# A fused AdaLN and routed low-rank FFN kernel: the first block's second stage in the two-level form of the others

## The chip, the cores and the metric

One core of one Trainium2 chip runs the whole kernel. The metric is the device time of one execution in microseconds (us), as a median over runs; smaller is better. Engines are called by the profile's names: PE is TensorE (matmul), DVE is VectorE, ACT is ScalarE, POOL is GpSimd, SP is SyncE (here a DMA queue only).

## The reference

Inputs are `x` (64 x 64 x 512), `cond` (64 x 256) and the weights, all fp32. Cut to what is computed:

```python
q = relu(cond @ W3 + b3)                          # one row of 512 per batch
v = (64 * x + x.sum(axis=1, keepdims=True)) * q[:, None, :]
y = relu(v @ W2 + b2)                             # first stage
base = y @ W_base + b_base                        # second stage
shared = (y @ A_s) @ B_s
gates = softmax(y @ W_router + b_router)          # 6 experts
w = the two largest gates, others 0
routed = sum over e of w[e] * (y @ A_r[e]) @ B_r[e]   # rank 16
out = x + base + shared + routed
```

## The kernel before

**Blocks.** The 4096 tokens are worked in four blocks (`k` = 0 to 3) of 1024. Features lie on partitions in four chunks of 128; a block's tokens are split into two halves of 512 columns. So v, y and the result of a block are each a 2 x 2 matrix of quarters: a pair of chunks by a half of the tokens (y11, y12 are the two chunk pairs of the first half, y21, y22 those of the second).

**Fewer products.** A product of 2 x 2 quarters is made with seven products instead of eight (Winograd's form): sums of quarters are formed first, four on the side of the rows (`row_sums`, L272) and four on the side of the weights (`weight_sums`, L134), then products numbered 1 to 7 are accumulated in PSUM. `seed` copies on ACT start a bank from another bank's value, since sums of products are shared. The same can be done once more inside a product: each of the seven is then itself made of seven products of 128 x 128 weights with 256 columns ("two levels"). It needs inner sums of both sides: `inner_row_steps` (L342) and `inner_weight_side` (L148), four instructions each.

**First stage.** Block 0 uses `first_mixed` (L397): plain products for half of the tokens and one level for the rest. It also starts block 1's preparation. Blocks 1 to 3 use `first_inner` (L480), two levels throughout.

**Second stage.** The loop at L1324 computes `ph`, which holds y's products with the low-rank and router weights. Then:
- block 0 calls `second` (L874): one level, seven products of four 512-column matmuls each, the routed part added in PSUM, x added by DVE out of PSUM, the result sent by SP's queue.
- blocks 1 and 2 call `second_between` (L714): products 1, 2, 4, 5 and 3 on two levels, products 6 and 7 on one. Products 6 and 7 are added to x on DVE and stored; the five others are left in SBUF by ACT copies and DVE additions and then added in DRAM by an accumulating DMA from POOL's queue (`to_rows`, L743).
- block 3 calls `second_inner`.

Inside, `gate` (L659) forms the softmax and the top two on DVE with one Exp on ACT, `weigh` (L636) multiplies them into `hw`, `turn` (L645) transposes `hw` on PE, and `difference` (L654) subtracts its halves on POOL. In `second_between` some products and their copies are issued between the gate's instructions (`first`, L793).

**Order by hand.** Every engine runs its instructions in the order in which the program issues them. The preparation of the next block (scaling x in place, 64 instructions on ACT, some on DVE; sums; row sums; inner sums) is cut into steps that wait in two lists: `behind`, drawn by `fill(n)`, and `held`, drawn by `sums_ahead(n)`. `prepare` (L302) fills the lists; for k = 1 it puts everything into `behind`, together with the sums of W_base (`tb_steps`) and part of the inner sums of W2 (`inner_steps[4:]`). In `second`, a helper `share` draws from `behind` in even portions. The inner sums of W_base are on POOL: `low_t` and `bcat_d` in `second` (the list `beside`), `wide["steps"]` around block 1's first stage.

Of the kernel before, what the change touches and what calls it, by code (L numbers as in the profile page):

```python
# [38 lines left out]
def adaln_ffn(ctx: ExitStack, tc: tile.TileContext, xa, x0, x1, head, w3, w2, wb, a, bcat, bb, br, outT):  # L39
# [80 lines left out]
    wb_sb = load_weight(wb, "wb_sb")  # L120
    bcat_sb = const.tile([GB, D], F32, tag="bcat_sb", name="bcat_sb")
    nc.sync.dma_start(bcat_sb[:GR], bcat)
    load_x(1)
    nc.sync.dma_start(bcat_sb[GR:], bb)
# [79 lines left out]
    def modulate(k):  # L204
# [18 lines left out]
        def batch(c, b):  # L223
            x = v[:, c, :, ts(b, NH)]
            scale, bias = nq[:, c, b : b + 1], vsum[:, c, b : b + 1]
            if k > 1 and c == CHUNKS[-1] and b >= BB // 2:
                nc.vector.tensor_scalar(x, x, scale, bias, ALU.mult, ALU.add)
            else:
                nc.scalar.activation(x, x, AF.Identity, bias=bias, scale=scale)  # L229
# [72 lines left out]
    def prepare(k, also=()):  # L302
# [8 lines left out]
        def row_step(c, n):  # L311
            if not made:
                ss[k], row_steps = row_sums(vs[k], "s")
                made.extend(
                    row_steps(slice(c, c + 1), nc.gpsimd if k > 1 and c == KH - 1 else nc.vector) for c in range(KH)
                )
            made[c][n]()
# [4 lines left out]
        among = [((4, 4 if k == 1 else 5), sums[c1])]  # L322
        if k == 1:
            among += [((25, 27, 29, 31), early), ((16, 16), sums[c2]), ((19, 20), sums[c3])]
        for places, steps in among:
            for n, step in reversed(list(zip(places, steps))):
                pairs[n].insert(0, step)
        for n, step in enumerate(also):
            pairs[n if n < 4 else 12 + n].append(step)
        behind.extend([step] for step in sums[c0])  # L330
        if k == 1:
            behind.extend(pairs)
            behind.extend([step] for step in late + prepare_inner(k))
        else:


            n = len(pairs) - BB // 4
            behind.extend(pairs[:n])
            first, inner_sums = prepare_inner(k, late[3])
            held.extend(sums[c2] + sums[c3] + early + first + sum(pairs[n:], []) + late[:3] + inner_sums)  # L340
# [9 lines left out]
    def prepare_inner(k, fourth=None):  # L350
# [30 lines left out]
        all_of, soon, third = slice(0, 4), slice(0, 3), slice(3, 4)  # L381
        late = []
        if fourth:
            late += [fourth] + steps("sums", of_s(third), nc.gpsimd, third)
            all_of = soon
        late += steps("two", of(0), nc.gpsimd)
        if fourth:
            late += [lambda: last_part.pop()()]
        late += steps("four", of(1), nc.gpsimd)
        inner[k] = dict(s=side, e3=lambda: s["e3"], places=late_places, late=late)  # L390
        inner_sums = steps("sums", of_s(all_of), nc.vector, all_of)
        return (first, inner_sums) if fourth else first + inner_sums
# [4 lines left out]
    def first_mixed(y):  # L397
# [52 lines left out]
        for step in t2_steps + inner_steps[:4] + s_steps():  # L450
            step()
        prepare(1, tb_steps + inner_steps[4:])
# [5 lines left out]
        for j in range(KH):  # L458
# [19 lines left out]
            fill(1)  # L478

# [220 lines left out]
    def load_rows(k):  # L700

        res = {}
        for n, (f, h) in zip(pair_tags[2:3] + pair_tags[:2] + pair_tags[3:], ((1, 0), (1, 1), (0, 0), (0, 1))):
            if (f, h) == (0, 0) and 0 < k < NB - 1:

                nc.sync.dma_start(outT[k, :KH, h], x1[k, :KH, :, ts(h, TB)])
                continue
# [6 lines left out]
    def second_between(k, y, res):  # L714
# [69 lines left out]
        for o in (1, 2):  # L784
            inner_sums(o)

        def main_part(ph):
            open_banks(1)
# [23 lines left out]
            fill(2)  # L812
            tools.take_u(1)
            sums_ahead(2)
            for j in range(KH):
                seed(j, "z", bank["y", j])
                with_x(x12, "y", j, KH, 0)
                if j == 0:
                    fill(2 if k == 1 else 1)

            for o in (5, 4):
                inner_sums(o)
            fill(2)
# [6 lines left out]
            fill(2)  # L830
# [5 lines left out]
            hws["less"] = difference(k, hwT)[:GB]  # L836
            inner_sums(3)
# [6 lines left out]
            fill(1)  # L844
# [4 lines left out]
            fill(1)  # L849
            sixth(3)  # L850
            fill(1)
# [3 lines left out]
            start(4)  # L855
            seventh(3)
            sums_ahead(2)
            second_and_third(3)
            sixth(4)
            ends(3)  # L860
# [12 lines left out]

    def second(k, y, ph, res):  # L874

        sy = sys_[k]
        ps = {}

        def bank(name, j):
            ps[name, j] = ps_p.tile([P, TB], F32, tag="pp", name=f"o{name}_{k}_{j}")  # L880
            return ps[name, j]

        def prod(i, j, name, start=True):
            product(bank(name, j) if start else ps[name, j], i, j, tb, sy, start=start)

        def seed(name, source, j):
            nc.scalar.copy(bank(name, j), ps[source, j])

        def row(f, h):
            return res[f // KH, h][:, f % KH]  # L890

        def with_x(name, j, f, h):

            t = row(f, h)
            nc.vector.tensor_tensor(t, ps[name, j], t, ALU.add)
            return t

        def routed(name, j, f, hw):
            nc.tensor.matmul(
                ps[name, j], bcat_sb[:, ts(f, P)], hw, start=False, stop=True, skip_group_check=True  # L900
            )

        def finish(name, j, f, h):
            nc.sync.dma_start(outT[k, f, h], with_x(name, j, f, h))

        def leave(p, f, h, add):
            nc.vector.tensor_tensor(add, p, add, ALU.add)
            nc.sync.dma_start(outT[k, f, h], add)


        places = list(range(9, 0, -1))
        most = {9: 4, 8: 5, 7: 6}

        def share():
            n = places.pop(0)
            left = len(behind) - 13
            fill(min(left, most.get(n, 6)) if left > 0 else -(-len(behind) // n))

        u12, u22 = {}, {}
        gate(k, ph)  # L920
        prod(1, 0, "x")
        seed("y", "x", 0)
        prod(1, 1, "x")
        seed("y", "x", 1)
        prod(6, 0, "y", start=False)
        seed("z", "y", 0)
        prod(2, 0, "x", start=False)
        weigh(k, ph)
        u12[0] = with_x("y", 0, KH, 0)
        share()  # L930
        prod(7, 0, "z", start=False)
        u22[0] = with_x("z", 0, KH, 1)
        prod(6, 1, "y", start=False)
        seed("z", "y", 1)
        u12[1] = with_x("y", 1, KH + 1, 0)
        share()
        prod(2, 1, "x", start=False)
        prod(7, 1, "z", start=False)
        u22[1] = with_x("z", 1, KH + 1, 1)
        hwT = turn(k)  # L940
        hwd = difference(k, hwT)
        for step in beside:
            step()
        share()
        prod(4, 0, "z", start=False)
        prod(5, 0, "w")
        share()
        routed("x", 0, 0, hwT[:GB, 0])
        finish("x", 0, 0, 0)
        routed("z", 0, 0, hwT[:GB, 1])  # L950
        finish("z", 0, 0, 1)

        routed("w", 0, KH, hwT[:GB, 1])
        leave(ps["w", 0], KH, 1, u22[0])
        share()
        prod(5, 1, "w")
        routed("w", 1, KH + 1, hwT[:GB, 1])
        leave(ps["w", 1], KH + 1, 1, u22[1])
        share()
        routed("x", 1, 1, hwT[:GB, 0])  # L960
        finish("x", 1, 1, 0)
        share()
        prod(4, 1, "z", start=False)
        routed("z", 1, 1, hwT[:GB, 1])
        finish("z", 1, 1, 1)
        share()
        prod(3, 0, "w", start=False)
        routed("w", 0, KH, hwd[:GB])
        leave(ps["w", 0], KH, 0, u12[0])
        share()  # L970
        prod(3, 1, "w", start=False)
        routed("w", 1, KH + 1, hwd[:GB])
        leave(ps["w", 1], KH + 1, 0, u12[1])
# [101 lines left out]
    def second_inner(k, y, res):  # L1075
# [196 lines left out]
    sys_, inner = {}, {}  # L1272
# [4 lines left out]
        w2_sb, t2, [(all_t[:, :, a:b], o, nc.vector) for a, b, o in ((0, 4, (5, 6, 7, 4)), (4, 6, (1, 2)), (6, 7, (3,)))]  # L1277
    )
    inner_steps = sum(inner_steps, [])
# [3 lines left out]
    low_side, low_steps = inner_weights(wb_sb, tb, [(low_t, (1, 2), nc.gpsimd)])  # L1283
# [3 lines left out]
    beside = [lambda: nc.gpsimd.tensor_tensor(bcat_d, bcat_pairs[:, :, 0], bcat_pairs[:, :, 1], ALU.subtract)]  # L1287
    beside += low_steps[0]
# [10 lines left out]
    for k in range(NB):  # L1299
# [5 lines left out]
        else:  # L1305
            if k == 1:
                for step in wide["steps"][0]:
                    step()
            rest = first_inner(k, y)
            if k == 1:  # L1310
                for step in wide["steps"][1]:
                    step()
# [10 lines left out]
        two = second_inner(k, y, res) if k == NB - 1 else second_between(k, y, res) if k else None  # L1323
        for n, (h, s) in enumerate(groups):  # L1324
            if rest and n == 0:
                sums_ahead(2)
            if rest and n == 2:
                rest()
                two["sums"]()
            if two and n in two:  # L1330
                if n == 6:
                    fill(4)
                two[n]()
                if n == 7:
# [6 lines left out]
        if two:  # L1341
            two["all"](ph)
            continue
        sys_[k], steps = row_sums(y, "sy")
        for step in steps():
            step()
# [53 lines left out]
```

## Time and profile before

The median of three runs is 253.76 us (252.5 to 253.93).

| | before |
|---|---|
| profiled execution, its own time | 253.81 us |
| its span in the trace | 252.0 us |
| TensorE's mean granted clock | 0.999 |
| busy: PE, DVE, ACT, POOL | 98%, 81%, 63%, 50% |
| block 0, second stage (window 34.21 to 73.15): busy PE, DVE, ACT, POOL | 38.94, 35.34, 23.59, 10.49 us of 38.94 |
| block 1, second stage (window 94.07 to 131.59): busy PE, DVE, ACT, POOL | 37.52, 35.47, 27.83, 22.56 us of 37.52 |

Times inside the trace count from the start of the span; the profiled execution lasted 1.8 us longer than its span. A line of a timeline gives the start, the length, the engine, the line of the kernel, the operation, what it writes from what it reads, the shapes and the count; the brackets at its end say how long the engine was idle before it and what ended that. The chain that ended last gives start, length and the work that set the pace there. A 4-byte matmul is recorded as two instructions.

### The profile page before, as it was taken

The page shows a single profiled execution, that of the slowest core. Times are in us where ns is not written, and L with a number is a line of the kernel's source. Part 1 is how long each engine was busy: PE and PEld are TensorE (multiplying, and loading weights), DVE is VectorE, ACT ScalarE, POOL GpSimd, SP SyncE. Part 2 cuts the span into 40 slices and gives each one's busy share as a digit, 9 for nine tenths or more (in the row PEclk, how much of TensorE's full clock was granted, in tenths as well). Part 3 has the DMA queues.
Part 4 walks back from the last instruction along what each step waited for, and adds up shares of the span by engine and source line. Part 5 has one row for each costly group of instructions (what it writes and reads, how often), then busy time and mean ns, then how long its engine had stood idle before and what let it go on. Part 6 is the DMA issues. An engine that isn't in the chain of part 4 may idle for free.

```text
span 252.0 us, 3678 instructions
## 1 busy us (share of the span) xinstructions
PE 246.8 (98%) x1134; PEld 189.4 (75%) x1134; DVE 203.8 (81%) x407; ACT 158.0 (63%) x436; POOL 126.2 (50%) x150
## 2 busy tenths in 40 slices
PE   8999999999999999999999999999999999999993
PEld 3846897454468889857888889947888889966783
DVE  2899998879996988999995778999992576797472
ACT  2299588579018889797638889796826428252310
POOL 1000000009707579059469968339659894059850
PEclk9999999999999999999999999999999999999999
DMA  6997818000431024835459922306259852500054
GB/s 181 370 350 274 330 28 307 0 3 16 151 125 42 3 86 138 336 147 216 61 80 195 156 94 101 127 25 250 28 79 197 138 133 97 166 1 0 9 194 134
DMA packets 17482, 33.82 MB, mean 134 GB/s; under 512 B 1605, under 2 KB 3781, under 8 KB 17462
## 3 DMA queue, kind: packets, MB, share of 16 engines
q1 hardware_dynamic: 13910, 27.09, 30.3%
q0 software_dynamic: 3264, 6.29, 15.9%
q10 hardware_dynamic: 288, 0.20, 0.3%
q8 instruction: 9, 0.15, 0.2%
q14 instruction: 11, 0.09, 0.1%
HBM read 19.94 MB, written 14.68 MB: 137 GB/s over the span
## 4 chain that ended last, share of the span: by engine, by line
PE 96%; DMA 2%; DVE 0%; SPq 0%; issue 0%
PE ia L502 14%; PE ph L1337 11%; PE ib L502 11%; PE ha L987 10%; PE hb L987 8%; PE oz L181 7%; PE py L409 6%; PE oy L181 6%; PE ja L987 4%; PE jb L987 3%; PE ox L181 3%; PE ow L181 3%; DMA w_sb<-in_w_dram 2%; PE yw L181 1%; PE pt L649 1%; PE yz L181 1%
## 5 line engine op out<-in xcount | busy, mean ns | idle before, releaser
L229 ACT ACTIVATE x<-x,vsum,nq 128x64 f32<-128x64 f32 x176 | 63.3, 431 | 1.4 <-DVE vsum L221 1.4
L656 POOL TENSOR_TENSOR hwd<-hwT 113x512 f32<-113x512 f32 x4 | 5.1, 1271 | 55.4 <-ACT hwT L651 55.4
L1337 PEld LDWEIGHTS ph<-a_sb,y 128*128 128x128 f32 x256 | 30.7, 192 | 0.8
L1337 PE MATMUL ph<-a_sb,y 128*128 128x118 f32 x256 | 30.7, 275 | 0.0
L493 DVE TENSOR_TENSOR u<-ib,u 128x256 f32<-128x256 f32 x42 | 16.4, 418 | 11.9 <-PE ib L502 11.8
L493 DVE TENSOR_TENSOR u<-ia,u 128x256 f32<-128x256 f32 (+1 forms) x36 | 16.1, 462 | 7.1 <-ACT u L540 5.8
L508 ACT COPY ib<-ia 128x256 f32<-128x256 f32 x21 | 7.6, 361 | 17.2 <-PE ia L502 17.2
L395 ACT ACTIVATE y<-u,head_sb 128x256 f32<-128x256 f32 (+1 forms) x30 | 15.8, 583 | 3.7 <-DVE u L468 3.0
L502 PE MATMUL ib<-inner_s,inner_t 128*128 128x256 f32 x60 | 17.4, 379 | 0.0
L219 DVE TENSOR_REDUCE vsum<-x 128x8 f32<-128x512 f32 x24 | 15.5, 676 | 0.0
L181 PE MATMUL oz<-sy,tb 128*128 128x512 f32 x32 | 15.0, 592 | 0.0
L409 PE MATMUL py<-v,w_sb 128*128 128x512 f32 (+1 forms) x40 | 14.4, 510 | 0.6 <-DMA w_sb<-in_w_dram 0.6
L181 PE MATMUL oy<-sy,tb 128*128 128x512 f32 x32 | 14.7, 597 | 0.0
L511 ACT COPY ib<-ib 128x256 f32<-128x256 f32 x21 | 7.6, 360 | 9.0 <-PE ib L502 8.6
L502 PEld LDWEIGHTS ib<-inner_s,inner_t 128*128 128x128 f32 x60 | 11.4, 190 | 1.6
L409 PEld LDWEIGHTS py<-v,w_sb 128*128 128x128 f32 x40 | 7.4, 190 | 6.7 <-issue 4.8
L344 POOL TENSOR_TENSOR sy<-sy 128x256 f32<-128x256 f32 x4 | 3.8, 952 | 17.2 <-PE oy L181 17.2
L267 ACT ACTIVATE v<-x,vsum,nq 128x64 f32<-128x64 f32 x32 | 11.0, 429 | 1.7 <-DVE vsum L265 1.7
L744 POOL DMA_DIRECT2D out_dram<-y x8 | 10.8, 1688 | 0.7 <-ACT ib L508 0.7
L181 PEld LDWEIGHTS oy<-sy,tb 128*128 128x128 f32 x32 | 5.8, 190 | 6.8 <-issue 6.2
L502 PE MATMUL ia<-s,t 128*128 128x256 f32 x36 | 10.2, 379 | 0.0
L181 PEld LDWEIGHTS oz<-sy,tb 128*128 128x128 f32 x32 | 5.8, 190 | 5.8 <-issue 5.3
(321 smaller groups left out, 679.9 us busy)
## 6 DMA issues: line engine op xcount, KB each, us to landing
xu<-in_x_dram SPq DMA_DIRECT2D x14, 512.0 KB, 4.4
out_dram<-xu SPq DMA_DIRECT2D x25, 256.0 KB, 2.2
x<-in_x_dram SPq DMA_DIRECT2D x12, 512.0 KB, 7.5
out_dram<-y POOLq DMA_DIRECT2D x8, 512.0 KB, 9.4
out_dram<-inner_tb POOLq DMA_DIRECT2D x4, 512.0 KB, 5.9
x<-in_x_dram SPq DMA_DIRECT2D x7, 256.0 KB, 5.7
w_sb<-in_w_dram SPq DMA_DIRECT2D x4, 256.0 KB, 5.5
wb_sb<-in_wb_dram SPq DMA_DIRECT2D x4, 256.0 KB, 5.0
```

Source lines behind the costliest of these rows:

```text
L181: nc.tensor.matmul(ps, w[i][:, c, ts(j, P)], s[i][:, c, :], start=start and c == 0, stop=c == KH - 1, skip_group_check=True,)
L219: nc.vector.tensor_reduce(vsum[:, c, bs], xc, AX.XY, ALU.add)
L229: nc.scalar.activation(x, x, AF.Identity, bias=bias, scale=scale)
L267: nc.scalar.activation(v[:, c, :, ts(b, NH)], batches_of(c, b, b + 1)[:, :, 0], AF.Identity, bias=vsum[:, c, b : b + 1], scale=nq[:, c, b ...
L395: nc.scalar.activation(y[:, f, h, cols], src, AF.Relu, bias=b2_sb[:, f : f + 1])
L409: nc.tensor.matmul(p[:, :, lo * NH : hi * NH], w2_sb[:, c, ts(f, P)], v[:, c, :, lo * NH : hi * NH], start=(c == 0 and lo == 0), stop=(c = ...
L493: add = lambda o, a, b: nc.vector.tensor_tensor(o, a, b, ALU.add)
L502: nc.tensor.matmul(bank[b, t][:, cols], t_side(o, n), s_side(o, n), start=n == 1, stop=True, skip_group_check=True,)
L508: nc.scalar.copy(bank["b", t][:, lo], bank["a", t][:, lo])
L744: nc.gpsimd.dma_start(outT[k, f : f + KH, h].rearrange("f p t -> p f t"), parts[o], accum_op=ALU.add)
L987: nc.tensor.matmul(p, w, s, start=start, stop=True, skip_group_check=True)
L1337: nc.tensor.matmul(ph[:, h * NS + s, :HC], y[:, c, h, ts(s, P)], a_sb[:, c, :], start=(c == 0), stop=(c == NC - 1),)
```

## The change

Block 0's second stage calls `second_between` like blocks 1 and 2, and `second` is gone (its 98 lines are left out below). With it:
- the inner sums of W2 for products 1, 2 and 3 (`plain_steps`, `third_steps`) go from DVE to POOL, as do the fourth row sum of one chunk and the inner sums of the third product in block 1's preparation; eight scalings of x go from ACT to DVE.
- all of POOL's weight sums are issued in block 0's second stage: `low_steps` between the inner sums of y11 and y12, the first group of `wide` at the start of the main part, then `third_steps`, `plain_steps` and `bcat_d`, the second group of `wide` later.
- `tb_steps` are issued behind the loop of `first_mixed` instead of within it.
- the load of W_base stands behind that of block 1's x; rows (0, 0) of block 0 are copied within DRAM from x, as in blocks 1 and 2.
- `held` has the `first` steps behind the last scalings, for all blocks; the counts for `fill` come from a list per block.

```diff
@@ loads
-    wb_sb = load_weight(wb, "wb_sb")
     bcat_sb = const.tile([GB, D], F32, tag="bcat_sb", name="bcat_sb")
     nc.sync.dma_start(bcat_sb[:GR], bcat)
     load_x(1)
+    wb_sb = load_weight(wb, "wb_sb")
@@ modulate
-            if k > 1 and c == CHUNKS[-1] and b >= BB // 2:
+            if c == CHUNKS[-1] and b >= BB // 2:
@@ prepare
-        if k == 1:
-            behind.extend(pairs)
-            behind.extend([step] for step in late + prepare_inner(k))
-        else:
...
-            held.extend(sums[c2] + sums[c3] + early + first + sum(pairs[n:], []) + late[:3] + inner_sums)
+        n = len(pairs) - BB // 4
+        behind.extend(pairs[:n])
+        first, inner_sums = prepare_inner(k, late[3])
+        held.extend(sums[c2] + sums[c3] + early + sum(pairs[n:], []) + first + late[:3] + inner_sums)
@@ first_mixed
-        for step in t2_steps + inner_steps[:4] + s_steps():
+        for step in t2_steps + inner_steps + s_steps():
             step()
-        prepare(1, tb_steps + inner_steps[4:])
+        prepare(1)
...
             relu(y, f1, 1, r1, other)
             fill(1)
+        for step in tb_steps:
+            step()
@@ load_rows
-            if (f, h) == (0, 0) and 0 < k < NB - 1:
+            if (f, h) == (0, 0) and k < NB - 1:
@@ second_between
-        for o in (1, 2):
-            inner_sums(o)
+        inner_sums(1)
+        if k == 0:
+            run(low_steps)
+        inner_sums(2)
+        pairs = list((2, 2 if k == 1 else 1, 2, 2, 1, 1, 1, 0, 0) if k else (2, 2, 3, 3, 2, 2, 1, 0, 0))
+        def weights(n):
+            if k == 0:
+                run(wide["steps"][n])
+                if n == 0:
+                    run(third_steps + plain_steps)
+                    nc.gpsimd.tensor_tensor(bcat_d, bcat_pairs[:, :, 0], bcat_pairs[:, :, 1], ALU.subtract)
         def main_part(ph):
+            weights(0)
             open_banks(1)
...
-            for o in (5, 4):
+            for o in (5, 4) if k else (4, 5):
                 inner_sums(o)
...
             hws["less"] = difference(k, hwT)[:GB]
+            weights(1)
             inner_sums(3)
@@ main loop
-            if rest and n == 0:
+            if n == 0:
                 sums_ahead(2)
-            if rest and n == 2:
-                rest()
+                fill(0 if rest else 6)
+            if n == 2:
+                if rest:
+                    rest()
                 two["sums"]()
...
-        sys_[k], steps = row_sums(y, "sy")
-        for step in steps():
-            step()
-        fill(9)
-        second(k, y, ph, res)
+        two["all"](ph)
```

## The prediction

> **What bounds the kernel now.** I read the page's shares first, then the chain that ended last, then the timelines of single engines around block 0's second stage. The page gives the bound in one line, and the chain shows it without a break through the stage that is changed:
>
> ```profile
> PE 246.8 (98%) x1134; PEld 189.4 (75%) x1134; DVE 203.8 (81%) x407; ACT 158.0 (63%) x436; POOL 126.2 (50%) x150
> ```
>
> ```profile
> 34.21 7.14 PE ph L1337 x64
> 41.35 3.44 PE ox L181 x8
> ...
> 55.09 0.87 PE pt L649 x8
> ...
> 72.29 0.86 PE ow L899 x2
> 73.15 1.73 PE ia L502 x8
> ```
>
> TensorE never stops from 34.21 to 73.15: block 0's second stage is 38.94 us of pure matmul time. The clock is 1.00 in every window of it. So only two things can move the time here: fewer matmul columns, or a wait that puts TensorE to sleep. The change does both.
>
> **Matmul time.** From the chain, a logical product of 512 columns takes 0.86 us (four in 3.44, two records each), one of 256 columns 0.43. Removed: 28 products of `second` (7 x 2 halves x 2 chunks) and 8 routed ones, 36 x 0.86 = 31.0 us. Added: 8 of 512 columns (o = 6, 7), 35 of 256 (five products of seven) and 16 routed of 256: 8 x 0.86 + 51 x 0.43 = 28.8. By count the gain is 2.2 us. Block 1 already runs this form: its chain goes from 94.07 to 131.59, 37.52 us, of which 0.44 is the first stage's leftover (`rest`). That is 37.08 against 38.94. I take 1.9 from the row. If nothing else waited, the stage would end at 34.21 + 37.08 = 71.29.
>
> **What VectorE must do before the gate.** In the new form TensorE depends on the gate early. ScalarE's queue holds the gate's Exp (L676) ahead of `take_w5(1)`, `take_11(0)`, `take_21(0)` and the seed of bank y; TensorE's first product of o = 6 waits for that seed. Block 1 shows how tight this is:
>
> ```profile
> 104.38 0.24 ACT L676 ACTIVATE g<-lg 128x48 f32<-128x48 f32 x1 [0.17 <-DVE lg L674]
> ...
> 105.98 0.59 ACT L754 COPY oy<-inner_tb 128x512 f32<-128x512 f32 x1
> ```
>
> ```profile
> 106.83 3.49 PE oy L181 x8
> ```
>
> The gate starts there at 103.67 (L669), Exp 0.71 later, and TensorE arrives at 106.83, 12.32 us into the stage net of the 0.44. The same place in block 0 is 34.21 + 12.32 = 46.53. In the old `second` nothing needs the gate before the transposes at 55.09, and the gate was done at 46.7 (L638, 45.65 + 1.09): 8 us of cover, which the change gives up.
>
> When can block 0's gate start? Today VectorE reaches it at 41.38, with the four row sums just in front:
>
> ```profile
> 36.13 1.22 DVE L280 TENSOR_TENSOR sy<-y 128x1024 f32<-128x1024 f32 x1
> ...
> 39.66 1.22 DVE L283 TENSOR_TENSOR sy<-y,sy 128x1024 f32<-128x1024 f32 x1
> 41.38 0.21 DVE L669 TENSOR_TENSOR lg<-ph,br_sb 128x48 f32<-128x48 f32 x1 [0.51 <-PE ph L1337]
> ```
>
> The four `tb_steps` ran between 29.6 and 34.5, in gaps in which VectorE waited for TensorE; now they stand behind the loop. Two reductions with their small product (L219, L221) also move ahead of the row sums (`sums_ahead(2)`). VectorE's queue from the last addition of the first stage (end 34.65) to the gate: reductions of chunk 2, 1.40 (34.73 to 36.13); `tb_steps`, 2.60 (the same shape for `t2` took 18.42 to 21.07); reductions of chunk 1, 1.40; row sums, 4.75 (36.13 to 40.88). 34.65 + 10.15 = 44.8, with GpSimd silent.
>
> **GpSimd is not silent.** It is idle until 57.16 today. The change fills it from 26.7 on: `inner_sums(1)` behind y11 (relu ends 26.65), `low_steps`, `inner_sums(2)` behind y12 (relu ends about 34.5), then in `weights(0)` the first group of `wide`, which waits for the last of `tb`, `third_steps` and `plain_steps` (8 instructions that VectorE did at 49.15 to 56.58), and `bcat_d`. Two rows show what VectorE pays when both engines read pairs of SBUF tensors:
>
> ```profile
> 156.24 1.22 DVE L280 TENSOR_TENSOR sy<-y 128x1024 f32<-128x1024 f32 x1 [1.08 <-ACT y L395]
> 157.50 1.64 DVE L281 TENSOR_TENSOR sy<-sy,y 128x1024 f32<-128x1024 f32 x1
> 159.06 1.75 DVE L282 TENSOR_TENSOR sy<-y 128x1024 f32<-128x1024 f32 x1
> ```
>
> ```profile
> 156.25 1.81 POOL L346 TENSOR_TENSOR inner_y<-y 128x256 f32<-128x256 f32 x1
> 158.02 1.71 POOL L347 TENSOR_TENSOR inner_y<-y,inner_y 128x256 f32<-128x256 f32 x1
> ```
>
> Each takes turns with the other: GpSimd's 0.73 us becomes 1.8, VectorE's 1.22 becomes 1.7. Additions out of PSUM (L895 at 0.68) and reductions (0.68) stay as they were. A row sum's pitch in block 1 grew from 1.14 to 1.84 (98.00 to 99.84): +0.70. A 512-element sum's grew from 0.60 to 1.13 (58.90 to 60.03): +0.53. A small L221 went from 0.17 to 0.41 to 0.96; I take +0.3. For a GpSimd instruction of 128 elements (0.46 alone) I take half of +0.70, an estimate.
>
> In the stretch before the gate: two of the four `tb_steps` meet the tail of `inner_sums(2)` (2 x 0.53); the other two run alone, since GpSimd waits for them; one L221 meets `wide` (0.3); two row sums meet `wide` (2 x 0.70) and two `third` (2 x 0.35). Together 3.46: the gate starts at 48.3. Bounds: 44.8 if nothing collides, 50.3 if all four `tb_steps`, both L221 and all row sums pay in full (2.1 + 0.6 + 2.8).
>
> The Trainium skill, SBUF — State Buffer, section "Who interferes with whom", says that a VectorE instruction with two SBUF inputs and a GpSimd instruction that reads SBUF hold one port pair in turn, the later one blocked for the other's whole duration. By the rule alone every meeting costs VectorE a full GpSimd instruction, about 0.7, and the `tb` term would be 1.4 instead of 1.06; the sum here goes by the rows. The rule speaks against putting GpSimd's work beside these sums at all.
>
> **From the gate to TensorE.** Exp follows after 0.71 plus 0.3 for L674's meeting, at 49.3. ScalarE then needs 0.15 + 3 x 0.27 + 0.52 + 0.1 for the wake-up, 1.6: TensorE resumes at 50.9 instead of 46.53, a new wait of 4.35 us. Bounds: 0.5 (gate at 44.8, L674 free) and 6.4 (gate at 50.3). What is late next: `hw`. Gate start to the end of L638 is 5.55 in block 1 (103.67 to 109.24); seven of its instructions read two SBUF tensors and meet `plain_steps`, `bcat_d` and `inner_sums(4)`, each +0.41 (L694 with GpSimd busy: 0.46 to 0.87). 48.3 + 5.55 + 2.9 = 56.75, while TensorE reaches the transposes at 50.9 + 3.49 + 1.72 = 56.1. I take 0.3, with 0 and 0.65 as bounds. From there VectorE keeps its distance of block 1: bank z is free about 62.5, where TensorE wants it for `start(3)`; 0 to 0.8, taken as nothing.
>
> **Edits costed at nothing.** ScalarE gains 30 copies of 256 elements (about 0.3 each) and loses 8 batches (0.34): some 29 us of 41, hidden by its idle time. The W_base load behind `load_x(1)` passes four 512 KB issues on SP's queue; all of both lands by about 24 (DMA share 0.53 in 22 to 24), `low_steps` needs it near 29.6. The margin is 5 us; beyond it each us delays GpSimd's line. `load_rows(0)` trades one load for a DRAM copy on SP. GpSimd's six accumulating DMAs cost its queue 1.2 to 2.5 each, and the second waits for the first, 5.4 (127.96); behind them stand only `fourth` and the sums for the third and second products of block 1's first stage, needed some 10 us into it. In block 1 the same queue met them by 4 us, here by about 3. `start(4)` needs `inner_sums(3)`, near 65 on GpSimd's queue, against 67.6. The reordered `held` list moves no work across stages.
>
> **Sum.** Stage end 71.29 + 4.35 + 0.3 = 75.94 against 73.15: +2.8 us. The profiled execution took 253.81 (span 252.0 and 1.8 around it), 0.05 above the median of 253.76. 253.8 + 2.8 = 256.6; I say 256.5.
>
> **Rivals.** *The gate is in time.* If GpSimd's meetings cost VectorE little (say its instructions fall among reductions and PSUM additions), the gate starts at 44.8, the wait is 0.5, and the stage ends at 71.8: 252.4. For it: TensorE's gain is certain, and today's row sums ran at 1.22 with the gate at once behind. Against: the 10.15 us in front of the gate are mostly two-input sums, and GpSimd has work for every one. It decides once the gate starts before 46.1, where wait and gain cancel; up to there 252.4 to 253.8, and not slower than before.
>
> *GpSimd's line is late too.* From 34.5 to the first instruction of `inner_sums(3)` it has 22 sums of 256 elements, 8 of 128 and the difference: at the shared 1.13, 0.85 and 1.27 that is 33 us, plus 1.9 waiting for `tb`: 69.4 instead of 65, 1.8 behind `start(4)`'s 67.6. 258.4, and each later sum would pace TensorE too. For it: GpSimd runs at its shared pace wherever VectorE is loaded. Against: VectorE's PSUM additions leave it half the time.
>
> *The wait is made up.* TensorE sleeps, but a later stage had a wait that shrinks, 253.8 again. Against: the chain is TensorE at 96% and shows no such wait.
>
> **Chances.** Forecast, 255.4 to 257.6: 0.55, split at 256.3 into slower 0.33 and same 0.22. Gate in time: 0.25, of which 0.03 beyond 1%. GpSimd late: 0.15, all slower. Made up: 0.05. A change of 1%, 2.5 us, is about what a measurement of this kernel tells from none. Slower 0.48, same 0.49, faster 0.03. The range leaves out a tenth at each side: from 252.6, just above the gate in time, to 258.8, just above GpSimd late.
>
> **What would show it.** Right: L669 of block 0 near 48, Exp behind it, TensorE idle some 4 us ahead of the first L181 of block 0 with ScalarE's seed as releaser; L280 to L283 of block 0 at 1.5 to 1.8 us; TensorE's busy time about 2 us lower. Wrong: the gate before 46, no idle in TensorE, or its idle placed at `start(3)` or `start(4)` behind VectorE or GpSimd.

## The result and the profile after

The changed kernel takes 256.47 us, the median of four runs (256.34 to 257.6); the kernel before, beside it, 253.7 (252.5 to 253.93). The ratio is 1.0133, with a 95% interval of 1.0112 to 1.0154. The profiled execution took 256.34 us, its span is 254.6, its clock 1.000. The prediction was 256.5.

From here on "the stage" is block 0's second stage, from the first `ph` product to the next stage's first product. It ran from 33.86 to 76.14, 42.28 us against 38.94 before. Block 1's second stage took 37.45 against 37.52. So the whole loss lies in the one stage that was changed, 3.3 us of it; the first stage ended 0.35 us earlier. In the page of after, the engines' busy times and then the shares of the chain that ended last:

```profile
PE 245.3 (96%) x1180; PEld 197.7 (78%) x1180; DVE 205.7 (81%) x410; ACT 165.1 (65%) x458; POOL 161.1 (63%) x189
...
PE 83%; DVE 15%; issue 1%; ACT 0%; DVEq 0%
```

TensorE has 1.5 us less to do, and yet the chain no longer runs on TensorE alone: 15% of it is VectorE's. The chain in order of time shows where (start, length, what set the pace):

```profile
32.98 0.88 PE yz L181 x4
33.88 0.42 DVE u L456
34.31 1.20 DVE vsum L219 x2
...
53.36 1.09 DVE hw L620
...
71.15 0.35 DVE y L881
71.54 2.00 PE hb L888 x8
```

It leaves TensorE at 33.88 and comes back at 71.54; in between there is nothing but VectorE and the short gaps between its instructions. The windows view of the stage says the same in busy time (PE, PEld, DVE, ACT, POOL):

```profile
33.86:76.14 42.28, 38.04 (x191) 29.88 (x191) 41.60 (x71) 30.15 (x88) 34.77 (x40) 1.00 0.39 107
```

VectorE is busy for 41.60 of 42.28 us. Before, TensorE was busy for all of 38.94 and VectorE for 35.34.

Where TensorE sleeps is in its timeline (the brackets give the idle time before and its releaser):

```profile
48.06 0.70 PE L888 MATMUL hb<-y,low_t 128*128 128x256 f32 x2 [3.61 <-DVE inner_tb L881]
...
60.93 0.70 PE L888 MATMUL hb<-y,low_t 128*128 128x256 f32 x2 [0.48 <-DVE inner_tb L881]
```

And why, in VectorE's timeline just ahead of it:

```profile
38.63 0.68 DVE L144 TENSOR_TENSOR tb<-wb_sb,tb 128x512 f32<-128x512 f32 x1
39.23 1.27 DVE L219 TENSOR_REDUCE vsum<-x 128x8 f32<-128x512 f32 x2
40.53 0.49 DVE L221 TENSOR_TENSOR vsum<-vsum,q_sb 128x16 f32<-128x16 f32 x1
40.94 1.21 DVE L280 TENSOR_TENSOR sy<-y 128x1024 f32<-128x1024 f32 x1
42.19 1.63 DVE L281 TENSOR_TENSOR sy<-sy,y 128x1024 f32<-128x1024 f32 x1
43.75 1.74 DVE L282 TENSOR_TENSOR sy<-y 128x1024 f32<-128x1024 f32 x1
45.41 1.47 DVE L283 TENSOR_TENSOR sy<-y,sy 128x1024 f32<-128x1024 f32 x1
46.80 0.20 DVE L651 TENSOR_TENSOR lg<-ph,br_sb 128x48 f32<-128x48 f32 x1
...
47.59 0.41 DVE L881 TENSOR_TENSOR inner_tb<-hb,inner_tb 128x256 f32<-128x256 f32 x1
```

The gate begins (L651) at 46.80, 5.4 us later than before (41.38). Behind its first three instructions stands `take_22(0)` (L881), which reads half of a PSUM bank out; the next product, `q(4, 0)`, writes that half, and TensorE, ready at 44.45, waits for it until 48.06. GpSimd's timeline shows who stretched the last three row sums:

```profile
40.26 0.73 POOL L152 TENSOR_TENSOR inner_tb<-tb,inner_tb 128x256 f32<-128x256 f32 x1
40.94 1.80 POOL L153 TENSOR_TENSOR inner_tb<-tb 128x256 f32<-128x256 f32 x1
42.70 1.70 POOL L154 TENSOR_TENSOR inner_tb<-tb,inner_tb 128x256 f32<-128x256 f32 x1
44.37 1.43 POOL L151 TENSOR_TENSOR inner_t<-w_sb 128x128 f32<-128x128 f32 x1
```

0.73 ahead of the row sums, 1.7 to 1.8 beside them. It looks as if the two engines take turns; the runs with writes in place of these sums (below) test it.

### The profile page after: what moved, and what is told of

Same layout as the page of the kernel before. It is cut to its first block, busy times and chain, and to the rows that moved or that the text cites. A ratio compares the mean times of both kernels' runs of the same rounds, so it can differ in the third digit from the quotient of the medians.

```text
span 254.6 us, 3851 instructions
## 1 busy us (share of the span) xinstructions
PE 245.3 (96%) x1180; PEld 197.7 (78%) x1180; DVE 205.7 (81%) x410; ACT 165.1 (65%) x458; POOL 161.1 (63%) x189
## 4 chain that ended last, share of the span: by engine, by line
PE 83%; DVE 15%; issue 1%; ACT 0%; DVEq 0%
PE ia L484 14%; PE ib L484 11%; PE ha L888 10%; PE hb L888 9%; PE ph L1233 8%; PE py L389 6%; PE ja L888 4%; PE oy L181 4%; PE oz L181 4%; PE jb L888 3%; DVE xu L881 2%; DVE vsum L219 1%; PE idle L192 1%; PE yw L181 1%; PE yx L396 1%; PE yz L181 1%
## 5 line engine op out<-in xcount | busy, mean ns | idle before, releaser
L229 ACT ACTIVATE x<-x,vsum,nq 128x64 f32<-128x64 f32 x168 | 61.3, 433 | 0.1
L331 POOL TENSOR_TENSOR inner_y<-y 128x256 f32<-128x256 f32 x11 | 8.2, 749 | 34.7 <-ACT y L375 34.7
L726 POOL DMA_DIRECT2D out_dram<-inner_tb x6 | 7.3, 1220 | 15.8 <-ACT y L904 15.8
L726 POOL DMA_DIRECT2D out_dram<-y x12 | 16.1, 1655 | 0.0
L331 POOL TENSOR_TENSOR sy<-sy 128x256 f32<-128x256 f32 x6 | 5.7, 953 | 16.1 <-PE oy L181 16.1
L881 DVE TENSOR_TENSOR xu<-oz,xu 128x512 f32<-128x512 f32 x16 | 10.5, 681 | 1.7 <-PE oz L181 1.6
L333 POOL TENSOR_TENSOR inner_y<-y 128x256 f32<-128x256 f32 x11 | 11.6, 1054 | 0.0
## 6 DMA issues: line engine op xcount, KB each, us to landing
out_dram<-xu SPq DMA_DIRECT2D x23, 256.0 KB, 2.2
x<-in_x_dram SPq DMA_DIRECT2D x7, 256.0 KB, 5.5
w_sb<-in_w_dram SPq DMA_DIRECT2D x4, 256.0 KB, 5.7
```

Of the source, the lines that this page charges most:

```text
L331: lambda: engine.tensor_tensor(to(0), a(0, 1), a(1, 1), ALU.add),
L726: nc.gpsimd.dma_start(outT[k, f : f + KH, h].rearrange("f p t -> p f t"), parts[o], accum_op=ALU.add)
L881: add = lambda o, a, b, engine=nc.vector: engine.tensor_tensor(o, a, b, ALU.add)
```

## The experiments

The questions: which part of the change makes the gate late? Does the meeting of VectorE and GpSimd cost what the trace suggests? What holds TensorE behind the gate? And where does TensorE's saved time go, if the gate is no longer late?

### The sums of W_base back into the first stage

```diff
-        prepare(1)
+        prepare(1, tb_steps)
 ...
-        for step in tb_steps:
-            step()
```

> The changed kernel, with the four tb_steps issued within the loop of first_mixed again, in VectorE's gaps there. Theory (the gate is late because of what VectorE has in front of it): the 3.47 us from 35.76 to 39.23 leave the queue, the gate starts near 43.3 instead of 46.8, the wait of 3.61 us at q(4, 0) falls to 0 to 0.3, the later 0.48 goes too; 252.3 to 252.8 us. Rival (GpSimd's sums beside VectorE's are the cost, wherever tb_steps stand): the gate still loses most of its time to them, 255 us or more. Rival (the two-level form costs block 0 by itself): 256.4.

Measured: 253.94 us against 253.54, ratio 1.0005 (0.9983 to 1.0026). The gate starts at 44.85, not 43.3, and the wait at `q(4, 0)` is 0.40 instead of 3.61. In TensorE's timeline:

```profile
32.93 1.13 PE L181 MATMUL yw<-s,w_sb 128*128 128x256 f32 x4 [0.44 <-DVE u L448]
...
45.92 0.70 PE L888 MATMUL hb<-y,low_t 128*128 128x256 f32 x2 [0.40 <-DVE inner_tb L881]
...
69.06 0.70 PE L888 MATMUL hb<-sy,inner_tb 128*128 128x256 f32 x2 [0.39 <-DVE y L881]
```

So the place of `tb_steps` accounts for 2.5 us, nearly the whole loss. But the gain that was to appear behind it (252.3 to 252.8) did not. The chain of this kernel tells why: it stands on VectorE from 30.80 on, apart from 1.15 us of first-stage products on TensorE at 32.93, and comes back to TensorE at the same wait as above:

```profile
30.80 0.41 DVE u L458
31.21 0.80 DVE tb L142
...
68.67 0.34 DVE y L881
69.06 2.00 PE hb L888 x8
```

VectorE's queue sets the stage's pace even with the loss undone: the stage takes 38.73 us (34.93 to 73.66), and VectorE is busy for 38.06 of them. That is 0.2 us less than before the change, and the first stage, in which TensorE waits 0.44, ends 0.7 us later than there.

### The same place in the kernel before

```diff
-        prepare(1, tb_steps + inner_steps[4:])
+        prepare(1, [lambda: None] * 4 + inner_steps[4:])
 ...
+        for step in tb_steps:
+            step()
```

> The kernel before, with only the tb_steps moved behind the loop of first_mixed, ahead of the row sums. Theory: the gate of the old second stage starts 2.5 us later, near 43.9, but TensorE asks for it only at the transposes at 55.1, so the time stays: 253.5 to 254.0 us. Rival (VectorE's throughput in the stage is the bound, not the early need of the gate): 255 us or more.

Measured: 253.73 us, ratio 1.0006 (0.9985 to 1.0028). Its row sums begin at 38.98 instead of 36.13, its gate at 43.64 instead of 41.38, and the stage takes 39.10 us instead of 38.94. The 0.16 us are lost where TensorE meets ScalarE's seed of its second bank, which `second` too has behind the gate's Exp:

```profile
44.36 0.24 ACT L678 ACTIVATE g<-lg 128x48 f32<-128x48 f32 x1 [1.65 <-DVE lg L676]
44.51 0.58 ACT L889 COPY oy<-ox 128x512 f32<-128x512 f32 x1
```

```profile
45.14 1.98 PE L181 MATMUL oy<-sy,tb 128*128 128x512 f32 x4
```

So the old form did need its gate ahead of the transposes: the cover on this path was about the 2.3 us by which the gate is late here, not the 8 us of the prediction. Up to there the late `tb_steps` cost next to nothing; they cost 2.5 us in the form that reads a bank of TensorE's behind the gate's first instructions.

### GpSimd writes but does not read

In place of the 13 sums of `weights(0)` GpSimd writes zeros; left out are the first group of `wide`, `third_steps`, `plain_steps` and `bcat_d`.

```diff
-                run(wide["steps"][n])
-                if n == 0:
-                    run(third_steps + plain_steps)
-                    nc.gpsimd.tensor_tensor(bcat_d, ...)
+                if n:
+                    run(wide["steps"][n])
+                else:
+                    for at in range(4):
+                        nc.gpsimd.memset(wide["place"][:, at, :2], 0.0)
 ...
```

> The changed kernel, with the 13 GpSimd sums of weights(0) replaced by memsets of the same places, so that they write and read nothing: left out are the first group of wide, third_steps, plain_steps and bcat_d. VectorE's queue ahead of the gate keeps its instructions. Theory: row sums fall back to a pitch of 1.14 to 1.25 (together 4.75 instead of 5.86), the gate starts near 45.5, its own sums lose nothing, the wait at q(4, 0) falls from 3.6 to about 2.3; 254.6 to 255.0 us, so contention is about a third of the loss. Rival (contention is all of it): 252.5 us, the wait gone. Rival (GpSimd is irrelevant): 256.4.

Measured: 257.08 us, ratio 1.0131 (1.0087 to 1.0175). The writes were done in 3.1 us, so `inner_sums(4)` moved up to 41.1 and met the row sums in place of the sums that were taken out: the gate at 46.86 again. So this run says nothing on the reads. That it took longer than the changed kernel goes with the clock: five of its six executions show a mean granted clock of 0.984 to 0.993 and took 256.88 to 257.9 us, the one at 1.000 took 255.8. The next run makes each write three times:

> The changed kernel with the GpSimd sums of weights(0) replaced by memsets as before, but each written three times over, so that GpSimd is busy for about as long (some 9 us, to 47 or so) and inner_sums(4) can't move up into the row sums. Left out are the first group of wide, third_steps, plain_steps and bcat_d. Theory (two engines reading SBUF take turns): row sums at 1.14 to 1.25, 4.75 us in all, the gate starts near 45.4 instead of 46.8, its own sums lose nothing until GpSimd reads again. Rival (any GpSimd work slows VectorE, writes too): row sums at 1.6 to 1.75, the gate at 46.8 again. The time is read with the clock beside it.

Measured: 254.14 us, ratio 1.0048 (1.0025 to 1.0071). VectorE's timeline:

```profile
40.53 1.22 DVE L280 TENSOR_TENSOR sy<-y 128x1024 f32<-128x1024 f32 x1
41.78 1.23 DVE L281 TENSOR_TENSOR sy<-sy,y 128x1024 f32<-128x1024 f32 x1
42.92 1.22 DVE L282 TENSOR_TENSOR sy<-y 128x1024 f32<-128x1024 f32 x1
44.05 1.22 DVE L283 TENSOR_TENSOR sy<-y,sy 128x1024 f32<-128x1024 f32 x1
45.19 0.20 DVE L651 TENSOR_TENSOR lg<-ph,br_sb 128x48 f32<-128x48 f32 x1
```

GpSimd is busy throughout, with writes alone:

```profile
38.00 3.10 POOL L784 MEMSET inner_tb<- 128x256 f32 x12
...
42.81 3.11 POOL L788 MEMSET inner_t<- 128x256 f32 x12
```

All four row sums are back at 1.22, the gate starts at 45.19, the wait at `q(4, 0)` is 1.92 and the one of after at 60.93 is down from 0.48 to 0.11. It is GpSimd's reads that VectorE pays for: 1.6 us at the gate, about 2.3 us of the time (the executions spread from 253.88 to 256.48). The parts overlap (this and the first experiment shorten the same queue), so 2.5 and 2.3 are not to be added. The Trainium skill, SBUF — State Buffer, section "Who interferes with whom", states that a VectorE instruction with two SBUF inputs contends with GpSimd's reads and not with its writes; the rows above agree.

### Two other orders

The first two steps of `held` (the reductions with L221) behind the gate for block 0:

```diff
-            sums_ahead(2)
+            sums_ahead(2 if k else 4)
 ...
-                sums_ahead(2)
+                sums_ahead(2 if rest else 0)
```

> The changed kernel, with block 0's first two steps of held (two reductions and their small product, 1.7 us) issued behind weigh with the next two instead of ahead of the row sums. Theory: the gate starts 1.7 us earlier, near 45.1, the wait at q(4, 0) falls to about 1.9, and VectorE does the same work later at no cost; 254.7 us. Rival (VectorE as a whole is the bound of the stage, so what leaves the front comes back behind): 256.0 or more, with a new wait at start(2) or start(3).

Measured: 255.75 us, ratio 1.0083 (1.0054 to 1.0113). The gate starts at 45.53, the wait is 2.03, but the profiled stage ends at 75.48, only 0.7 us ahead of after's 76.14. What left VectorE's queue ahead of the gate came back behind it, and in this execution the clock fell after the wait. The time lies between the two theories, and the clock is not what kept it from 254.7: the two executions at a clock of 0.999 and 1.000 took 255.46 and 255.47. The windows view of the profiled one (granted clock third from the end):

```profile
48.00:50.00 2.00, 2.00 (x5) 1.30 (x4) 1.97 (x4) 2.00 (x6) 1.92 (x3) 0.50 0.13 51
50.00:52.00 2.00, 2.00 (x5) 0.92 (x4) 1.83 (x4) 0.78 (x3) 2.00 (x4) 0.73 0.11 41
```

The products and reads that wait behind the gate, issued ahead of it instead:

```diff
-            gate(k, ph, (first, lambda: tools.take_12(0)))
+            if k == 0:
+                first()
+            gate(k, ph, ((lambda: None) if k == 0 else first, ...))
```

> The changed kernel, with block 0's products and copies of first issued ahead of the gate instead of between its third and fourth instruction. It tells which tie holds TensorE: the bank that take_22(0) reads, or the gate's Exp in front of ScalarE's copies. Theory (the bank, behind VectorE's row sums, is held first; Exp's path is next by less than half a us): take_22(0) runs directly behind the row sums at 46.8, 0.8 us earlier, and ScalarE's copies no longer stand behind Exp: the wait at q(4, 0) falls from 3.6 to about 2.8; 255.6 to 256.0 us. Rival (Exp alone holds TensorE, as the prediction had it): the wait disappears, 253.5 us or less. Rival (the gate's lateness reaches the transposes anyway): 256.4 with the wait moved there.

Measured: 256.77 us, ratio 1.0142 (1.0123 to 1.0162), no better than after. The wait at `q(4, 0)` falls to 2.82, as the theory had it, since the read stands ahead of the gate; so it was this read that held TensorE. Its time of 255.6 to 256.0 did not come: the gate is later (47.23), the second product of bank y waits 0.47 for ScalarE's seed, and VectorE itself waits 0.47 for Exp:

```profile
51.60 1.98 PE L181 MATMUL oy<-sy,tb 128*128 128x512 f32 x4 [0.47 <-ACT oy L736]
```

```profile
48.65 0.20 DVE L661 TENSOR_REDUCE sm<-g 128x8 f32<-128x48 f32 x1 [0.47 <-ACT g L658]
```

The lateness only changed its place.

### Both moves together, and what stays then

The sums of W_base in the loop and the reductions behind the gate:

> The changed kernel with both of VectorE's blocks out of the way of the gate: the tb_steps within the loop of first_mixed, and the two reductions of block 0's held list behind weigh. The tb_steps alone brought the gate to 44.85 and the wait at q(4, 0) to 0.4 us; the reductions are 1.39 us more. Theory: the gate starts near 43.5, before TensorE needs it, the wait at q(4, 0) is gone, and with it all risk for the clock; TensorE's gain shows: 252.9 to 253.4 us, 0.2 to 0.6 under the kernel before (the 0.44 us that the first stage loses to tb_steps remain). Rival (VectorE's whole load bounds the stage): the same 253.9 as with tb_steps alone, with waits at later places.

Measured: 254.03 us against 253.47, ratio 1.0019 (1.0009 to 1.0029). The gate starts at 43.14 and there is no wait at `q(4, 0)`. The stage takes 38.94 us (34.61 to 73.55), as before the change. Its waits now stand later:

```profile
53.54 1.98 PE L181 MATMUL oz<-sy,tb 128*128 128x512 f32 x4 [0.52 <-ACT oz L736]
...
68.95 0.70 PE L888 MATMUL hb<-sy,inner_tb 128*128 128x256 f32 x2 [0.35 <-DVE y L881]
```

The first is the seed of bank z on ScalarE, behind scalings of x that wait for the reduction moved. No one engine carries the chain here: it runs on TensorE to 44.4, VectorE to 52.2, ScalarE to 56.0, TensorE to 62.4 and VectorE to 68.9, and VectorE is busy for 37.5 of the 38.94 us. So ScalarE's scalings were drawn later, on top of both moves:

```diff
-  ... if k else (2, 2, 3, 3, 2, 2, 1, 0, 0))
+  ... if k else (2, 1, 2, 3, 3, 3, 1, 0, 0))
```

> The kernel with the sums of W_base within the first stage and the reductions behind the gate, with block 1's scalings of x drawn later: 2, 1, 2, 3, 3, 3, 1 pairs instead of 2, 2, 3, 3, 2, 2, 1. Theory (the gain is lost in small waits for ScalarE, whose queue has scalings, one of them waiting for a reduction on VectorE, ahead of the seed of the second bank z and of the copies of hwT): the waits of 0.52 at the second product of o=7 and of 0.24 and 0.12 at hwT go, the others (0.44 in the first stage, some 0.5 before the stage's end behind VectorE) stay. Stage 38.1 instead of 38.94, time 253.1 to 253.4, 0.9985 of the kernel before. Rival (the loss is VectorE's queue as a whole, which reaches its PSUM additions late whatever ScalarE does): TensorE comes earlier and waits at the next bank instead: 253.9 to 254.1, and the wait at a PSUM addition of VectorE grows from 0.35 to 0.8 or more.

Measured: 254.69 us, ratio 1.0037 (1.0024 to 1.005): slower, as the rival had it, but by more than its 254.1, and the wait grew at other places than the one it named.

```profile
58.39 0.70 PE L888 MATMUL hb<-y,low_t 128*128 128x256 f32 x2 [0.61 <-DVE inner_tb L881]
63.15 0.67 PE L888 MATMUL hb<-sy,inner_tb 128*128 128x256 f32 x2 [0.61 <-ACT hb L896]
```

The waits for the seed and for `hwT` are gone; TensorE meets VectorE's read at 58.39 and, at 63.15, a copy of ScalarE that now has six scalings ahead of it.

In addition, the sums of W2 into GpSimd's idle 5 us between its first two accumulating DMAs:

```diff
                 run(wide["steps"][n])
-                if n == 0:
-                    run(third_steps + plain_steps)
 ...
             to_rows(1, 0, 0)
+            if k == 0:
+                run(third_steps + plain_steps)
             to_rows(2, 0, 0)
```

> As the other of this pair, and GpSimd's sums of W2 for products 1, 2 and 3 (eight instructions) go from ahead of the gate's end into the 5 us in which GpSimd waits between its first two accumulating DMAs. Theory (turns on SBUF reads are what VectorE loses in this stage): inner_sums(4) and (5) move up by 5 us and meet VectorE in the gate in place of the sums that left, so VectorE gains little; inner_sums(3) ends near 59 instead of 64; no change against the other, 253.1 to 253.4. Rival (the sums of W2 cost VectorE time that nothing else would): hw some 0.7 us earlier, and 252.7 to 252.9.

Measured: 258.5 us, ratio 1.0204 (1.018 to 1.0227). Both theories missed. GpSimd's idle time there was the time in which VectorE worked undisturbed. VectorE's inner sums of x from 65.85 to 69.1 now take 0.72 to 0.94 instead of 0.42, its read behind them is late, and TensorE waits:

```profile
72.03 0.91 PE L889 MATMUL hb<-sy,inner_tb 128*128 128x256 f32 x2 [2.63 <-DVE y L882]
```

Behind this wait the clock falls: in the chain the eight matmul records (four products) from 72.03 take 3.47 us, where the kernel without this edit has 2.00. Longer wait (2.63 instead of 0.28) and lower clock are about the difference of 3.8 us.

### Work taken from VectorE

The last eight scalings of block 1's x, which the change had given to VectorE, back on ScalarE, in three kernels: with the sums in the loop, with both moves, and in the changed kernel alone.

```diff
-            if c == CHUNKS[-1] and b >= BB // 2:
+            if k > 1 and c == CHUNKS[-1] and b >= BB // 2:
```

> The change with the sums of W_base within the first stage's loop, and besides with the last eight scalings of block 1's x back on ScalarE, as before the change. Theory (in block 0's second stage the chain that ended last now runs on VectorE's queue without a break, from 30.8 to 69.1 with the sums in the loop; whatever leaves that queue shortens the stage, until TensorE's own 37 us bind): 3.4 us leave it near 61 to 65, the 0.39 wait behind VectorE at 69 goes, with the wait of 0.4 at q(4,0) staying: stage 38.3 to 38.5 instead of 38.96, time 253.2 to 253.5, a little below or at the kernel before. Rival (ScalarE has no room there either: its queue is full from 57 to 66 with copies that TensorE's banks need): the wait moves to a copy of ScalarE: 253.9 to 254.5.

> As the kernel with both moves (sums of W_base in the loop, the first two reductions behind the gate), and the last eight scalings of block 1's x back on ScalarE. Theory (VectorE's queue is the bound of the stage): the 0.35 wait at 69 behind VectorE goes, the waits behind ScalarE (0.52 at o=7, 0.36 at hwT) stay: 253.5 to 253.7 against 254.0. Rival (ScalarE has no room): 254.0 to 254.6.

> The changed kernel with one part undone: the last eight scalings of block 1's x on ScalarE again. Theory (VectorE's queue sets the stage's length from 34 to 71.5: 41.6 us busy of 42.3): the wait of 3.61 ahead of the gate stays as it is, since the scalings come behind it, but what TensorE waits after it (0.48 and two of about 0.1, each with some 0.27 for the restart) shrinks at the last place: 255.9 to 256.2 instead of 256.4. Rival (the gate alone sets the loss and the rest runs at TensorE's pace): no change, 256.3 to 256.5. Second rival (ScalarE has no room): 256.5 to 257.

Measured: 255.27 us (ratio 1.0083, 1.0054 to 1.0111), 255.46 (1.0079, 1.0066 to 1.0091) and 259.32 (1.0243, 1.0217 to 1.0269): 1.3, 1.4 and 2.9 us slower than the same kernels without the edit. The theory fell in all three; that ScalarE has no room had the direction, but each loss is larger than its range. (The 38.96 in the first of these expectations counts the last 0.23 us of the first stage; 38.73 is right. The 0.27 for a restart in the last one stands in no row; the restarts of after cost some 0.1.) In the timeline of ScalarE of the last:

```profile
66.88 0.36 ACT L904 COPY y<-ha 128x256 f32<-128x256 f32 x1
67.14 3.09 ACT L229 ACTIVATE x<-x,vsum,nq 128x64 f32<-128x64 f32 x9
70.13 0.37 ACT L899 COPY hb<-hb 128x256 f32<-128x256 f32 x1
```

Nine scalings in a row hold back the copies that empty TensorE's banks; its timeline shows who waits:

```profile
67.08 0.67 PE L888 MATMUL hb<-sy,inner_tb 128*128 128x256 f32 x2 [0.56 <-ACT hb L896]
71.01 0.70 PE L888 MATMUL hb<-sy,inner_tb 128*128 128x256 f32 x2 [0.66 <-ACT y L904]
```

VectorE now waits up to 3.40 us for ScalarE (L881 at 71.91), and the sums of x behind it are late all the same. So of the two places tried the eight scalings are better on VectorE in this form, and the busy share of ScalarE (30 of 42 us) did not show that it was full in this stretch. In the changed kernel alone the profiled execution lost another 1.6 us to the clock behind the 3.61 wait: the eight records of bank y took 4.70 us instead of 3.49, the four ahead of them 1.29 instead of 0.86.

None of these kernels beats the kernel before. The nearest are the two with the loss undone, 253.94 and 254.03, the old time again to within 0.2%.

## Why the prediction came out where it did

**The number and the cause.** 256.5 was forecast and 256.47 measured, by the forecast case: GpSimd's sums and the moved `tb_steps` make the gate late, and TensorE sleeps ahead of it by more than its products save. The first experiment shows the part of `tb_steps` (2.5 us), the writes without reads that of GpSimd's reads (2.3); the two overlap. But the close agreement is partly luck, since terms that were off cancelled. The prediction had a stage of 37.08 + 4.35 + 0.3 = 41.73; measured, by starts, are 37.0 of TensorE's work, 3.88 lost ahead of the gate, nothing at the transposes and 1.4 at later places, 42.28. The first stage, which the prediction took as it was, ended 0.35 earlier and gave that much back.

**The gate's time.** Forecast 48.3, measured 46.80. The first stage ended 0.35 earlier. `tb_steps` with the meetings took 3.47 (39.23 − 35.76) against 3.66. The reductions with L221 took what was forecast. The row sums took 5.86 (46.80 − 40.94), where the prediction had 4.75 + 2.1 = 6.85: the first one lost nothing and the last 0.25. The mis-sized term is this 2.1; it measured 1.1.

**The releaser.** The prediction named the seed of bank y, through Exp and ScalarE's copies, 2.6 us behind the gate's start. The wait stands at `q(4, 0)`, one product group earlier, and its releaser is `take_22(0)` on VectorE itself. That is the step of the prediction that failed: I followed the copies in ScalarE's queue and did not ask which reads of VectorE's own stand behind the gate's first instructions. The named path was only just hidden: the seed ended at 49.79 and the product that needs it started at 49.89 (though a copy ahead of the seed, at 48.79, had itself waited 0.31 for one of the late products). The gate came 1.5 us earlier than forecast. But bank y's first product followed it by 3.1 us instead of 2.6, and TensorE could have been there at 46.0 instead of 46.53: 4.35 − 1.5 + 0.5 + 0.5 is about the 3.88 by which it was late.

**What is late next.** The 0.3 at the transposes was not paid: `hw` was done at 54.45, the transposes began at 55.09. Instead TensorE's products at 60.93 and 71.54 started 0.65 and 0.32 late, behind VectorE's reads, and the one at 65.04 0.12 late, just behind ScalarE's seed of that bank (it ended at 64.89), where the prediction had taken 0 to 0.8 as nothing; and each restart costs some 0.1 (0.53 from the product at 48.06 to the next, 0.43 between others).

**TensorE's gain.** 1.9 was taken, and it is there. Without a wait the starts of two products of 256 columns lie 0.43 apart. By this measure, restarts included, TensorE loses 3.88 at 48.06, 0.75 at 60.93, 0.19 at 65.04, 0.06 at 66.41 and 0.43 at 71.54 (the brackets give less, 3.61 and 0.48 for the first two, since they count from the end of the product before). 42.28 less these 5.31 leaves 37.0, against 38.94; the first experiment leaves the same 37.0 of its 38.73. This is worked out from starts and not tried by itself. TensorE's busy time on the page fell by 1.5 (246.8 to 245.3), where the prediction looked for about 2.

**The rivals.** *GpSimd late* fell: `inner_sums(3)` ended at 65.7 and TensorE never waited for GpSimd. *The gate in time* did not come, but its price can be read against the kernels that make it so: it said 252.4 to 253.8 for a gate before 46.1, and with the gate at 43.14 and 44.85 the time was 254.0 and 253.9. So even an early gate gives no gain. The prediction took the stage as TensorE's time plus one wait; TensorE then runs into VectorE's queue, of about the old stage's length, and with the gate at 43.14 into ScalarE's as well. *Made up* was wrong in its reason: nothing later gave the loss back (the span grew by 2.6).

**What stays open.** That VectorE's queue bounds the stage at about 39 us is read from the chains (with both moves ScalarE has a part in it) and from what shortened or stretched that queue (reads removed, reads added). The one try to take work off it, the eight scalings, moved the bound to ScalarE. A kernel with less work on VectorE and none of it elsewhere in this stretch was not run, so how far TensorE's saving could be had is not known.

## What to carry to other kernels

When a form saves matmul time by more additions and copies, compare each other engine's busy time in that stage with the new, shorter stage before you look at single waits: 35.3 us of VectorE under 38.9 of TensorE left no room here for a TensorE of 37 when the new form brings VectorE to 38.1, as in the first experiment. For a moved step, look up every read of PSUM that is queued behind it, the engine's own included, and which matmul writes that bank next. In these runs GpSimd's idle time beside a loaded VectorE was not free, unless GpSimd only wrote there.

## What the runs showed of the hardware

**The clock after a wait.** A sleep of TensorE can cost more than its length. Behind a wait of 2.03 us the granted clock fell to 0.50 in one 2 us window and 0.73 in the next (shown above); behind 3.61 us in the changed kernel with the scalings on ScalarE the windows view has

```profile
50.00:52.00 2.00, 2.00 (x4) 1.08 (x4) 1.97 (x5) 1.88 (x6) 2.00 (x3) 0.50 0.13 49
52.00:54.00 2.00, 2.00 (x4) 0.76 (x3) 1.83 (x4) 0.90 (x4) 1.92 (x3) 0.70 0.01 3
```

and behind the same 3.61 us in the profiled execution of after it stayed at 1.00. The two lower clocks among after's other runs were 0.992 (256.39 us) and 0.984 (257.6); with the scalings on ScalarE all six runs have 0.987 to 0.993. What a lower clock costs in time differs: with the reductions behind the gate 255.46 and 255.47 stand against 255.58 to 256.69, with GpSimd's short writes 255.8 against 256.88 to 257.9. The prediction had left this out.

The Trainium skill, TensorE: Matmul & The Clock Gate, section "Part 1: The HAM clock gate", gives an idle window of about 3.4 us, free-running, as what throttles. That the same wait did and did not lower the clock fits a free-running window. But 2.03 us is shorter than the page's figure, and there the measurement decides: the clock fell all the same.

**Small instructions pay most for their size.** Beside GpSimd's sums a 16-column product (L221) went from 0.17 to 0.49 and the 288-column `eq` (L672) to 1.02, where the run with both moves has 0.63. A short instruction can last until the other engine's is over: L221 ends at 41.02, the GpSimd sum that was running when it began (40.26, 0.73) at 40.99.
